# An AdaLN transformer block on one core: the last layernorm transposed by VectorE and DMAs, both down projections of the first batch in a row, and two more warm-up tiles

## Chip, cores and metric

The kernel runs on one core of one Trainium2 chip. The metric is the device time of one execution in microseconds. The reading units are the five engines of the core: TensorE (PE, with its weight loads as PEld), VectorE (DVE), ScalarE (ACT), GpSimd (POOL) and SyncE (SP, which here only issues DMAs).

## The reference

Two batches of 1024 rows of 256 numbers go through an attention block and a feed-forward block, both behind a layernorm that a small product of the condition `c` shifts and scales. Everything is float32. There are 16 heads of 128, causal masking, and a hidden size of 704 in the feed-forward part.

```python
mod = (silu(c) @ wmod).reshape(2, 6, 1, 256)
sa, ca, ga, sb, cb, gb = (mod[:, i] for i in range(6))
ga = (2 * (ga >= 0) - 1) * maximum(abs(ga), 0.25)       # gb likewise
h = layernorm(x) * (1 + ca) + sa
x = x + ga * attention(h, Wq, bq, Wk, bk, Wv, bv, Wo, bo)   # rotary q and k, causal
h = layernorm(x) * (1 + cb) + sb
gate, up = h @ Wgate.T, h @ Wup.T                       # W = (wq - 128) * scale per row
x = x + gb * ((silu(gate) * up) @ Wdown.T)
```

## The kernel before

All of it is written out by hand in one order: within `tc.manual_schedule()` each engine executes its instructions as the program emits them, and the framework adds only the semaphores. So the place of a call in the text is its place in the queue of every engine that it uses.

**Start.** `warm_up(n)` issues one product of a matrix of ones into a scratch bank of PSUM (`warm_ps`), n tiles of 128 columns wide; nobody reads it. There is one `warm_up(4)` before the condition arrives, and `warm_up(4)` and `warm_up(2)` behind the tiny transpose `pc` of the condition. Then `modulation(0)` multiplies the condition with the weights `wmod` (tile `pm`, line 125) as they land, and `ln_turn` transposes the first layernormed rows on TensorE (tile `ptx_a`, line 218); `gates_product` (`pg`) and the projections `pq`, `pk`, `pv` follow.

**Middle.** 32 units, one for each batch and head, are computed one after the other. A unit has eight steps of 128 query rows: scores (`ps`), softmax, and the probabilities turned. That turning is done without TensorE: VectorE transposes 32x32 blocks into the buffer `t32[blk]`, and 16 DMAs from SP move the blocks to their places in `pT` (tags `pT0` and `pT1`). The products with the values (`po`), the output projection (`py`) and the next unit's q, k, v are put between the steps. `project_out` multiplies one row tile and VectorE adds it to `x` (line 521).

**Layernorm.** It consists of `ln_stats`, `ln_sqrt` and `ln_scale` (result `xn`), and then one of two ways to turn rows into columns. `ln_turn` uses eight TensorE transposes for each block of 512 rows, into PSUM, and VectorE applies shift and scale while draining. The other way, which the second batch's first layernorm and the first batch's second one use, is `ln_move` (VectorE, 32x32 blocks), `ln_send` (16 DMAs on SP for both blocks) and `ln_shift` (shift and scale on POOL). The last layernorm, the one of batch 1 before the feed-forward part, uses `ln_turn`.

**Feed-forward and tail.** For each batch `b` and block `blk` of 512 rows, `hidden(b, blk, c)` makes one of six chunks of 128 hidden features (tile `pgu`, in a pair of banks of the pool `ps_sc`), ScalarE applies silu, and VectorE multiplies gate and up into `gT`. With `hold=True` that multiplication is put off until the next `owed.pop()()`. The last chunk holds 64 gate and 64 up features. `down(b, blk)` multiplies `gT` with the down weights for four row tiles: `chunks` are the 128-row products (tile `pd`, line 606), `halves` the 64-row products of the last chunk (line 596), alternately from the upper and the lower half of the partitions. `store` adds `x` on VectorE (tile `yo`, line 622) and sends the rows out by SP (line 623). Before the change `halves` come after the chunks, except in the very last `down`, where they come first.

Late `py` tiles and the `pd` tiles take their bank from `bank()`, in rotation over four entries:

```python
banks = [(ps_y, "y"), (ps_a, "a"), (ps_a, "a"), (ps_o, "o")]
```

`ps_o` with its single bank also holds `po`, so `values` waits until the last late `py` there has been drained.

The tail after the 32 units is a plain sequence: the four chunks of hidden(0, 1) between the last output projections, the statistics of the first four row tiles of batch 1, the last `values`, then hidden(0, 1, 4), four projections, hidden(0, 1, 5), the transposes of block 0 of the last layernorm, down(0, 0), and hidden(1, 0) with the transposes of block 1 behind its first chunk and down(0, 1) behind its fourth; then hidden(1, 1) with down(1, 0) in it, and down(1, 1).

Of the kernel before, what the change touches and what calls it, by code (L numbers as in the profile page):

```python
# [11 lines left out]
F32 = mybir.dt.float32  # L12
# [5 lines left out]
P = 128  # L18
B, S, D = 2, 1024, 256
H, DH = 16, 128  # L20
HID = 704
NT = S // P
KC = D // P
HG = 2
NG = H // HG
NF = (HID + P - 1) // P
FULL = (HID // P) * P
QB = 512
NB = S // QB
# [8 lines left out]
def adaln_block(ctx: ExitStack, tc: tile.TileContext, a, cos_d, sin_d, out):  # L38
    nc = tc.nc
# [7 lines left out]
    ps_a = pool("ps_a", 2, space=PSUM)  # L47
    ps_o = pool("ps_o", 1, space=PSUM)
    ps_y = pool("ps_y", 1, space=PSUM)
# [36 lines left out]
    def warm_up(tiles):  # L86
        some = ones.unsqueeze(1).to_broadcast([P, tiles, P])
        nc.tensor.matmul(warm_ps[:, : tiles * P], ones, some, start=True, stop=True)
# [108 lines left out]
    def ln_scale(b, name, blk, part=range(4)):  # L197
        mv, rstd = stats[b, name]
        part = [4 * blk + j for j in part]
        some = slice(part[0], part[-1] + 1)  # L200
        nc.vector.reciprocal(rstd[:, some], rstd[:, some])
        for t in part:
            xn = xnp.tile([P, D], F32, tag="xn", name=f"xn_{name}{b}_{t}")
            nc.vector.tensor_scalar(
                xn, x[b][:, t, :], mv[:, t, 0:1], rstd[:, t : t + 1], ALU.subtract, ALU.mult
            )
            xns[b, name, t] = xn
# [19 lines left out]

    moved = {}

    def ln_move(b, name, t):  # L230

        if t == 0:
            moved[b, name] = [
                fpool.tile([P, 4, NB, KC, 4, 32], F32, tag="f", name=f"xt{n}_{name}{b}") for n in range(2)
            ]

        nc.vector.transpose(
            moved[b, name][0][:, :, t // 4, :, t % 4, :].rearrange("p c f q -> p f c q"),
            xns[b, name, t].rearrange("p (f c a) -> p f c a", c=4, a=32),
        )  # L240

    def ln_send(b, name, cs):
        src, dst = moved[b, name]
        for c in cs:
            for r in range(4):
                nc.sync.dma_start(dst[ts(c, 32), r], src[ts(r, 32), c])

    def ln_shift(b, name, blk, which, dest, f):
        nc.gpsimd.tensor_scalar(
# [231 lines left out]
    def values(u, blk, k0, k1):  # L481
        b, g, h = u
        if blk == 0 and k0 == 0:
            outs[u] = opool.tile([P, S], F32, tag="o", name=f"o_{b}{g}{h}")
        if k0 == 0:
            pos[u, blk] = ps_o.tile([P, 512], F32, tag="o", name=f"po_{b}{g}{h}{blk}")
        po = pos[u, blk]
        last = 4 * blk + 3
        pT = pTs[u, blk].rearrange("p r i k b -> p i r k b")
        for k in range(k0, k1):  # L490
            off = max(0, k - 4 * blk)
            nc.tensor.matmul(  # L492
                po[:, off * P :],
                vs[b, g][:, k, ts(h, DH)],
                pT[:, off:, :, k, :],
                start=(k == 0),
                stop=(k == last),
            )
        if k1 == last + 1:
            nc.scalar.copy(outs[u][:, ts(blk, QB)], po)  # L500

    banks = [(ps_y, "y"), (ps_a, "a"), (ps_a, "a"), (ps_o, "o")]
    turn = [0]

    def bank(name):

        pool, tag = banks[turn[0] % 4]
        turn[0] += 1
        return pool.tile([P, 512], F32, tag=tag, name=name)

    def project_out(u, t, late=False):

        b, g, h = u
        if t % 4 == 0:
            nc.vector.reciprocal(rdens[u][:, t : t + 4], dens[u][:, t : t + 4])
        name = f"py_{b}{g}{h}{t}"
        py = bank(name) if late else ps_y.tile([P, 512], F32, tag="y", name=name)
        nc.tensor.matmul(  # L518
            py[:, :D], outs[u][:, ts(t, P)], weights[b, g]["o"][:, h, :], start=True, stop=True
        )  # L520
        nc.vector.scalar_tensor_tensor(  # L521
            x[b][:, t, :], py[:, :D], rdens[u][:, t : t + 1], x[b][:, t, :], ALU.mult, ALU.add
        )
# [4 lines left out]
    def new_h2(b, blk):  # L528

        tag = (f"hT{blk}", f"cs{blk}")[b]  # L530
        h2s[b, blk] = hpool.tile([P, KC, QB], F32, tag=tag, name=f"h2_{b}{blk}")
        return h2s[b, blk]

    def hidden(b, blk, c, late=True, first=None, hold=False):
        if c == 0 if first is None else first:
            gTs[b, blk] = fpool.tile([P, NF, QB], F32, tag="f", name=f"gT_{b}{blk}")
        last = c == NF - 1
        if late:
            pg = ps_sc.tile([P, S], F32, tag="sc", name=f"pgu_{b}{blk}{c}")
            pgs = [pg[:, ts(j, QB)] for j in range(2)]  # L540
        else:
            pgs = [
                ps_a.tile([P, 512], F32, tag="a", name=f"pgu_{b}{blk}{c}{j}") for j in range(2 - last)
            ]
        for pg, n in zip(pgs, ("gate",) if last else ("gate", "up")):
            for k in range(KC):
                nc.tensor.matmul(  # L547
                    pg,
                    wT["last"][:, k, :] if last else wT[n][:, k, ts(c, P)],
                    h2s[b, blk][:, k, :],  # L550
                    start=(k == 0),
                    stop=(k == KC - 1),
                )
        sg = ppool.tile([P, QB], F32, tag="p", name=f"sg_{b}{blk}{c}")

        rest = (last_gate_up if last else full_gate_up)(b, blk, c, sg, pgs)
        if hold:
            owed.append(rest)
        else:
            rest()  # L560
# [19 lines left out]
        nc.scalar.activation(sg, pgs[0], AF.Silu)  # L580
        return lambda: nc.vector.tensor_tensor(gTs[b, blk][:, c, :], sg, pgs[1], ALU.mult)

    def down(b, blk):

        end = (b, blk) == (1, 1)
        pds = [bank(f"pd_{b}{blk}{j}") for j in range(4)]

        parts = [(j, pds[j], slice(0, D)) for j in range(4)]
        if end:
            rest = ps_sc.tile([P, S], F32, tag="sc", name=f"pd_{b}{blk}r")  # L590
            parts[3:] = [(3, pds[3], slice(0, P)), (3, rest, slice(P, D))]

        def halves():
            for j, pd, cols in parts:
                half = ts(j % 2, HID - FULL)
                nc.tensor.matmul(  # L596
                    pd[:, cols],
                    gTs[b, blk][half, NF - 1, ts(j, P)],
                    wdT[b][half, NF - 1, cols],
                    start=end,  # L600
                    stop=not end,
                )

        def chunks(j, pd, cols):
            for c in range(NF - 1):
                nc.tensor.matmul(  # L606
                    pd[:, cols],
                    gTs[b, blk][:, c, ts(j, P)],
                    wdT[b][:, c, cols],
                    start=(c == 0 and not end),  # L610
                    stop=(c == NF - 2 and end),
                )

        def store(j, pd, cols):
            t = blk * 4 + j
            if cols.start == 0:
                if (b, blk) == (0, 0):
                    yos[t] = rot.tile([P, D], F32, tag="r1", name=f"yo_{b}{t}")
                else:
                    yos[t] = xnp.tile([P, D], F32, tag="xn", name=f"yo_{b}{t}")  # L620
            yo = yos[t]
            nc.vector.tensor_tensor(yo[:, cols], pd[:, cols], x[b][:, t, cols], ALU.add)
            nc.sync.dma_start(out[b, ts(t, P), cols], yo[:, cols])

        yos = {}
        if end:

            halves()
            for part in parts:
                chunks(*part)  # L630
                store(*part)
            return
        for part in parts:
            chunks(*part)
        halves()
        for part in parts:
            store(*part)
# [62 lines left out]
    with tc.manual_schedule():  # L700
        pc = ps_a.tile([P, 512], F32, tag="a", name="pc")
        nc.tensor.transpose(pc[:, : B * KC], row_c, ident[: B * KC, : B * KC])
        warm_up(4)
        warm_up(2)
        nc.scalar.activation(sc.rearrange("p b k -> p (b k)"), pc[:, : B * KC], AF.Silu)
        nc.scalar.activation(warm, eps_t, AF.Sqrt)
        weights[0, 0] = {}
# [97 lines left out]
            ln_stats(1, "b", t)  # L805
        ln_sqrt(1, "b", 0, 4)
        values(u, 1, 0, 8)
        ln_scale(1, "b", 0)
        hidden(0, 1, 4)
        for t in range(4, NT):  # L810
            project_out(u, t, late=True)
        hidden(0, 1, 5)
        ln_turn(1, "b", 0, 2, new_h2(1, 0), wide=True)
        for t in range(4, NT):
            ln_stats(1, "b", t)
        ln_sqrt(1, "b", 4, NT)
        ln_scale(1, "b", 1)
        down(0, 0)
        for c in range(NF):
            hidden(1, 0, c)  # L820
            if c == 0:
                ln_turn(1, "b", 1, 2, new_h2(1, 1))
            if c == 3:
                down(0, 1)
        order = (NF - 1, *range(NF - 1))
        for c in order:
            hidden(1, 1, c, first=(c == order[0]))
# [69 lines left out]
```

## Time and profile before

| | us |
|---|---|
| three runs, median (lowest to highest) | 1075.6 (1075.38 to 1075.73) |
| the profiled execution, its own time | 1076.84 |
| its span, first to last instruction | 1075.1 |

| engine | busy us | share of the span | instructions |
|---|---|---|---|
| PE | 1070.5 | 100% | 3529 |
| DVE | 655.1 | 61% | 1423 |
| ACT | 507.7 | 47% | 956 |
| POOL | 396.1 | 37% | 364 |

The page shows one profiled execution. Busy time is the time that an engine has an instruction in it; a float32 product of TensorE is recorded as two matmul instructions, and consecutive matmuls overlap in the records by their pipeline's depth (0.16 us at full speed), so that what one product costs in a row of them is read from the distance of the starts, or from the chain of work that ended last, which counts each instruction up to the next. Register, branch and DMA-issuing instructions are not counted as busy. A wait is put down to the last semaphore event before it.

### The profile page before, as it was taken

Reading aid. Unit: us, or ns where it says so; the run is one execution under the profiler, and the core shown is the slowest. Engines: PE = TensorE matmul, PEld = TensorE weight load, DVE = VectorE, ACT = ScalarE, POOL = GpSimd, SP = SyncE. Lnnn points to the kernel's source line nnn. Section 1 sums busy time; section 2 is a strip of 40 time slices with the busy share of each in tenths; the row PEclk is TensorE's granted clock in tenths of the full one; section 3 lists DMA queues with packets and bytes.
Section 4 is the critical chain, followed back from the end, with each engine's and each line's share of the span. In section 5 each row is a group of like instructions: output and inputs, shape, how many; then the busy total and the mean of one; then the engine's idle time right before and its main releaser. Section 6 shows DMA issues by size and latency. Waiting matters only on the chain.

```text
span 1075.1 us, 12364 instructions
## 1 busy us (share of the span) xinstructions
PE 1070.5 (100%) x3529; PEld 641.4 (60%) x3529; DVE 655.1 (61%) x1423; ACT 507.7 (47%) x956; POOL 396.1 (37%) x364
## 2 busy tenths in 40 slices
PE   9999999999999999999999999999999999999998
PEld 5656555666666655555666656655555666555656
DVE  5656665666767776665666566666677765544421
ACT  4654544554445544544554444444454554562110
POOL 3825353534343343754332443324343433100000
PEclk9999999999999999999999999999999999999999
DMA  6465655657565555565554656454555556432001
GB/s 218 96 161 126 161 119 135 164 127 181 118 152 112 142 117 134 122 149 126 112 148 109 147 113 155 101 139 99 139 114 126 143 128 137 103 69 49 20 20 40
DMA packets 66656, 130.99 MB, mean 122 GB/s; under 512 B 18806, under 2 KB 22010, under 8 KB 66588
## 3 DMA queue, kind: packets, MB, share of 16 engines
q1 hardware_dynamic: 64804, 125.78, 49.4%
q10 hardware_dynamic: 1736, 4.29, 1.2%
q8 instruction: 29, 0.48, 0.2%
q14 instruction: 39, 0.32, 0.1%
q0 software_dynamic: 48, 0.13, 0.1%
HBM read 25.26 MB, written 2.10 MB: 25 GB/s over the span
## 4 chain that ended last, share of the span: by engine, by line
PE 99%; DMA 0%; DVE 0%; SPq 0%; issue 0%
PE po L492 23%; PE ps L431 23%; PE pv L370 10%; PE pq L388 10%; PE py L518 10%; PE pk L388 10%; PE pgu L547 7%; PE pd L606 3%; PE pm L125 1%; DMA wmod<-in_wmod 0%; PE pd L596 0%; PE ptx_a L218 0%; PE pg L149 0%; PE ptx_b L218 0%; PE pd_11r L606 0%; DVE x L521 0%
## 5 line engine op out<-in xcount | busy, mean ns | idle before, releaser
L451 ACT ACTIVATE p<-ps,nmax 128x128 f32<-128x128 f32 (+7 forms) x256 | 189.8, 741 | 342.7 <-DVE nmax L434 342.3
L431 PE MATMUL ps<-kT,qT 128*128 128x512 f32 (+3 forms) x768 | 289.5, 486 | 0.0
L434 DVE CUSTOM_DVE_ANT_0 ps<-ps,mask 128x128 f32<-128x128 f32 (+7 forms) x256 | 195.5, 764 | 114.5 <-PE ps L431 113.6
L492 PE MATMUL po<-pT,v 128*128 128x512 f32 (+3 forms) x768 | 263.7, 486 | 0.1
L521 DVE SCALAR_TENSOR_TENSOR x<-py,rden,x 128x256 f32<-128x256 f32 x256 | 122.7, 481 | 220.6 <-PE py L518 216.8
L492 PEld LDWEIGHTS po<-pT,v 128*128 128x128 f32 x768 | 145.7, 190 | 123.9 <-issue 92.8
L401 POOL TENSOR_TENSOR r_q<-r_q,sin_t 128x512 f32<-128x512 f32 x64 | 81.9, 1280 | 364.5 <-ACT r_q L400 348.9
L465 DVE STREAM_TRANSPOSE t<-p 128x128 f32<-128x128 f32 (+7 forms) x256 | 198.2, 774 | 3.6 <-DMA pT<-t 1.8
L431 PEld LDWEIGHTS ps<-kT,qT 128*128 128x128 f32 x768 | 145.7, 190 | 77.6 <-issue 64.1
L518 PE MATMUL py<-wo,o 128*128 128x256 f32 x512 | 151.2, 380 | 0.0
L518 PEld LDWEIGHTS py<-wo,o 128*128 128x128 f32 x512 | 92.6, 190 | 77.6 <-issue 53.1
L370 PE MATMUL pv<-wv,hT 128*128 128x256 f32 x512 | 121.1, 379 | 0.0
L388 PE MATMUL pq<-hT,wq 128*128 128x512 f32 x256 | 120.5, 593 | 0.0
L388 PE MATMUL pk<-hT,wk 128*128 128x512 f32 x256 | 120.3, 592 | 0.0
L370 PEld LDWEIGHTS pv<-wv,hT 128*128 128x128 f32 x512 | 94.8, 190 | 19.5 <-issue 1.3
L401 POOL TENSOR_TENSOR r_k<-r_k,sin_t 128x512 f32<-128x512 f32 x64 | 81.5, 1273 | 64.4 <-ACT r_k L400 64.4
L407 POOL TENSOR_TENSOR kT<-kT,r_k 128x512 f32<-128x512 f32 x64 | 81.2, 1269 | 55.8 <-DVE kT L404 41.1
L400 ACT ACTIVATE r_q<-pq,cols 64x512 f32<-64x512 f32 x128 | 87.4, 683 | 22.3 <-PE pq L388 19.8
L407 POOL TENSOR_TENSOR qT<-qT,r_q 128x512 f32<-128x512 f32 x64 | 83.7, 1308 | 33.9 <-DVE qT L404 29.7
L400 ACT ACTIVATE r_k<-pk,cols 64x512 f32<-64x512 f32 x128 | 87.4, 683 | 6.4 <-PE pk L388 1.0
L388 PEld LDWEIGHTS pk<-hT,wk 128*128 128x128 f32 x256 | 48.6, 190 | 48.0 <-issue 44.2
L388 PEld LDWEIGHTS pq<-hT,wq 128*128 128x128 f32 x256 | 46.2, 190 | 33.1 <-issue 30.6
(96 smaller groups left out, 691.3 us busy)
## 6 DMA issues: line engine op xcount, KB each, us to landing
pT<-t SPq DMA_DIRECT2D x512, 128.0 KB, 2.4
pT<-t SPq DMA_DIRECT2D x512, 64.0 KB, 2.0
wq<-in_Wq SPq DMA_DIRECT2D x16, 256.0 KB, 3.0
wk<-in_Wk SPq DMA_DIRECT2D x16, 256.0 KB, 4.1
wv<-in_Wv SPq DMA_DIRECT2D x16, 256.0 KB, 4.1
wo<-in_Wo SPq DMA_DIRECT2D x16, 256.0 KB, 2.9
out<-yo SPq DMA_DIRECT2D x15, 128.0 KB, 1.8
wmod<-in_wmod SPq DMA_DIRECT2D x4, 256.0 KB, 5.5
```

The costliest lines, as they stand in the source:

```text
L370: nc.tensor.matmul(pv[:, ts(j, HG * DH)], hT[b, n][:, k, ts(r, P)], weights[b, g]["v"][:, k, :], start=(k == 0), stop=(k == KC - 1),)
L388: nc.tensor.matmul(pq, weights[b, g][s][:, k, ts(h, DH)], hT[b, n][:, k, :], start=(k == 0), stop=(k == KC - 1),)
L400: nc.scalar.activation(r1[to], pq[of], AF.Identity, bias=cols[of, c : c + 1])
L401: nc.gpsimd.tensor_tensor(r1, r1, sin_t[:, sl], ALU.mult)
L407: nc.gpsimd.tensor_tensor(dst[:, sl], dst[:, sl], r1, ALU.add)
L431: nc.tensor.matmul(ps[:, c:e], qT[:, ts(i, P)], kT[:, c:e], start=True, stop=True)
L434: nc.vector.tensor_tensor_reduce(ps[:, :L], ps[:, :L], mask[:, NT - 1 - i :, :].rearrange("p t k -> p (t k)"), -SCALE, FLT_MAX, ALU.add, A ...
L451: nc.scalar.activation(p[:, :L], ps[:, :L], AF.Exp, bias=nmax, scale=-1.0, accum_out=dens[u][:, i : i + 1])
L465: nc.vector.transpose(t32[blk][:, :, j, : i + 1, :].rearrange("p c k b -> p k c b"), p[:, : (i + 1) * P].rearrange("p (k c a) -> p k c a", ...
L492: nc.tensor.matmul(po[:, off * P :], vs[b, g][:, k, ts(h, DH)], pT[:, off:, :, k, :], start=(k == 0), stop=(k == last),)
L518: nc.tensor.matmul(py[:, :D], outs[u][:, ts(t, P)], weights[b, g]["o"][:, h, :], start=True, stop=True)
L521: nc.vector.scalar_tensor_tensor(x[b][:, t, :], py[:, :D], rdens[u][:, t : t + 1], x[b][:, t, :], ALU.mult, ALU.add)
```

## The change

- The last layernorm (batch 1, before the feed-forward part) is turned by `ln_move`, `ln_send` and `ln_shift` instead of `ln_turn`. `ln_move` gets buffers from the caller: the block transposes go into `t32[0]`, and a new tile in the pool slot `pT0` receives the DMAs. `ln_send` can send one block alone: 16 DMAs for block 0 behind the first four block transposes, and 16 more for block 1 behind down(0, 0)'s stores. In all there are 32 DMAs of 32 partitions x 256 elements, eight block transposes and four POOL instructions; 16 TensorE transposes and four VectorE drains go.
- down(0, 1) moves from behind hidden(1, 0, 3) to right behind down(0, 0). It takes two pairs of banks of `ps_sc` (`wide`) and does its 64-row products first (`first`), so that the 64-row products of down(0, 0) and down(0, 1) stand together.
- The multiplication of hidden(0, 1, 4) is held until the four output projections have been emitted.
- In the rotation of banks the third and the fourth entry change places.
- The two warm-up products behind `pc` are both four tiles wide: eight tiles instead of six.

```diff
-    def ln_move(b, name, t):
+    def ln_move(b, name, t, room=None):
         if t == 0:
-            moved[b, name] = [
+            moved[b, name] = room or [
...
-    def ln_send(b, name, cs):
+    def ln_send(b, name, cs, blks=slice(NB)):
         src, dst = moved[b, name]
         for c in cs:
             for r in range(4):
-                nc.sync.dma_start(dst[ts(c, 32), r], src[ts(r, 32), c])
+                nc.sync.dma_start(dst[ts(c, 32), r, blks], src[ts(r, 32), c, blks])
...
-    banks = [(ps_y, "y"), (ps_a, "a"), (ps_a, "a"), (ps_o, "o")]
+    banks = [(ps_y, "y"), (ps_a, "a"), (ps_o, "o"), (ps_a, "a")]
...
-    def down(b, blk):
+    def down(b, blk, wide=False, first=False):
         end = (b, blk) == (1, 1)
-        pds = [bank(f"pd_{b}{blk}{j}") for j in range(4)]
+        first = first or end
+        if wide:
+            pairs = [ps_sc.tile([P, S], F32, tag="sc", name=f"pd_{b}{blk}{j}") for j in range(2)]
+            pds = [pair[:, ts(j, QB)] for j in range(2) for pair in pairs]
+        else:
+            pds = [bank(f"pd_{b}{blk}{j}") for j in range(4)]
...
-                    start=end,
-                    stop=not end,
+                    start=first,
+                    stop=not first,
...
-        if end:
+        if first:
             halves()
...
-        warm_up(4)
-        warm_up(2)
+        for n in range(2):
+            warm_up(4)
...
         values(u, 1, 0, 8)
+        room = [t32[0], ptpool.tile([P, 4, 4, 4, 32], F32, tag="pT0", name="xt_b1")]
+        room = [
+            t.rearrange("p c a b q -> p (c a b q)").rearrange(
+                "p (c n f j q) -> p c n f j q", c=4, n=NB, f=KC, j=4
+            )
+            for t in room
+        ]
         ln_scale(1, "b", 0)
-        hidden(0, 1, 4)
+        for t in range(4):
+            ln_move(1, "b", t, room)
+        ln_send(1, "b", range(4), slice(0, 1))
+        hidden(0, 1, 4, hold=True)
         for t in range(4, NT):
             project_out(u, t, late=True)
+        owed.pop()()
         hidden(0, 1, 5)
-        ln_turn(1, "b", 0, 2, new_h2(1, 0), wide=True)
         for t in range(4, NT):
             ln_stats(1, "b", t)
         ln_sqrt(1, "b", 4, NT)
         ln_scale(1, "b", 1)
+        for t in range(4, NT):
+            ln_move(1, "b", t)
         down(0, 0)
+        for f in range(KC):
+            ln_shift(1, "b", 0, 2, h2s[1, 0] if f else new_h2(1, 0), f)
+        ln_send(1, "b", range(4), slice(1, 2))
+        down(0, 1, wide=True, first=True)
+        for f in range(KC):
+            ln_shift(1, "b", 1, 2, h2s[1, 1] if f else new_h2(1, 1), f)
         for c in range(NF):
             hidden(1, 0, c)
-            if c == 0:
-                ln_turn(1, "b", 1, 2, new_h2(1, 1))
-            if c == 3:
-                down(0, 1)
```

More of the change, by code (lines that the diff above doesn't have):

```diff
@@ L609, in chunks @@
                     wdT[b][:, c, cols],
-                    start=(c == 0 and not end),
-                    stop=(c == NF - 2 and end),
+                    start=(c == 0 and not first),
+                    stop=(c == NF - 2 and first),
                 )
```

## The prediction

> **What bounds the kernel now.** I read the page's engine table first, then the chain that ended last, then the timelines of the first 22 us and of the last 120 us. The page says that TensorE (PE) is the bound:
>
> ```profile
> span 1075.1 us, 12364 instructions
> PE 1070.5 (100%) x3529; PEld 641.4 (60%) x3529; DVE 655.1 (61%) x1423; ACT 507.7 (47%) x956; POOL 396.1 (37%) x364
> ```
>
> No other engine is above 61%. So a PE product taken away is worth its full pitch, and work given to DVE, POOL or SP costs nothing until PE waits for it. The chain over the last 136 us (start, duration, engine and tile; a product here is two matmul instructions) shows that PE hardly waits:
>
> ```profile
> 978.73 0.45 PE py L518 x2
> 979.18 0.03 issue
> 979.20 0.93 DVE x L521 x2
> 980.13 0.04 issue
> 980.17 5.86 PE po L492 x16
> ...
> 992.91 0.87 PE ptx_b L218 x8
> 993.78 8.63 PE pd L606 x40
> 1002.42 1.06 PE pd L596 x8
> 1003.48 3.63 PE pgu L547 x8
> 1007.11 0.87 PE ptx_b L218 x8
> ```
>
> The reader is to see three things. The eight transposes of each block (ptx_b) stand in the chain, at 0.109 us each. The 64-row products (L596) and the first hidden products behind them (3.63 us, where eight otherwise take 3.44) carry a surcharge. And one hop leaves PE: po waits for DVE's update of x.
>
> The other place is the start. In PE's timeline:
>
> ```profile
> 3.33 2.93 PE L88 MATMUL warm_ps<-ones 128*128 128x512 f32 x4
> 6.79 3.75 PE L125 MATMUL pm<-sc,wmod 128*128 128x128 f32 x16 [0.54 <-DMA wmod<-in_wmod]
> 10.33 1.45 PE L218 MATMUL ptx_a<-ident,xn_a 128*128 128x128 f32 x8
> ...
> 17.93 1.04 PE L218 MATMUL ptx_a<-ident,xn_a 128*128 128x128 f32 x8
> ```
>
> Sixteen pm instructions begin over 3.54 us, 0.213 us apart; the transposes at 17.93 are 0.109 apart. So PE runs at half speed until a switch. The eight transposes at 10.33 take 0.41 us more than their twins at 17.93, which is four slow ones (4 x 0.104): the switch is at about 10.33 + 4 x 0.213 = 11.2 us. The warm-ups stop 0.5 to 0.7 us before pm.
>
> **What the Trainium skill says.** (1) "TensorE: Matmul & The Clock Gate", Part 1: PE starts at half clock and is released after one busy window of about 3.4 us; windows run freely and do not restart with the kernel. The trace agrees on half and full pitch (0.213, 0.109); no view shows the windows themselves. (2) "TensorEngine Tiling (Array Packing)", Key Properties: a change of tiling mode drains TensorE. The trace agrees: a stretch of eight 64-row instructions costs 1.06 us and 0.19 on the products behind it, 1.25; they start as four pairs 0.209 apart (0.84), so entering and leaving costs 0.41. (3) "VectorE: DVE Perf Modes", The three transpose paths: VectorE transposes 32x32 blocks only, so DMAs must move the blocks; the kernel already does so for xt_a and xt_b, and its rows give the prices:
>
> ```profile
> L237 DVE STREAM_TRANSPOSE xt_b<-xn_b x8: 395/430/433, 814.6 to 855.1; 128x256 f32<-128x256 f32 x8
> L246 SPq DMA_DIRECT2D xt_a<-xt_a x16: 534/589/1371, 391.3 to 424.9; - x16
> L246 SPq DMA_DIRECT2D xt_b<-xt_b x16: 534/588/590, 860.2 to 893.9; - x16
> L249 POOL TENSOR_SCALAR h<-xt_b,modT x4: 769/772/779, 911.9 to 919.0; 128x512 f32<-128x512 f32 x4
> ```
>
> **The change, part by part.** Times below are the trace's, before any gain.
>
> *A. Transposes off PE.* 16 x 0.109 = **-1.75 us**, all in the chain. Their replacements: on DVE, 8 block transposes x 0.43 = 3.4 us, for four drains (4 x 0.8) that go. The first four stand behind the scaling (ends 985.2), end about 986.8, and are ahead of the four x updates, whose products come from 989.5: no delay. The hidden product held (hidden(0,1,4)) is multiplied after those updates, about 992.4; it is needed at 1003. The second four follow block 1's scaling (about 998.5 to 1000.2), write the half of t32_0 that the first sends do not read, and are done before the first store of down(0,0), about 1002.8. On SP, 16 sends x 0.588 = 9.4 us: 986.8 to 996.2, landing +2.0 (xt_b's landing), POOL 2 x 0.77: h2_10 is ready at 999.8. It is needed when hidden(1,0,0) begins: down(0,0) at 992.7, plus 8.63, plus 16 half products 2.1, plus 8.63, is 1012. Slack 12 us. Block 1: its sends wait on SP behind four output stores, of which two wait for a buffer (before: until 1005.4, end 1006.3); 1006.3 + 9.4 + 2.0 + 1.55 = 1019.3, needed at 1012 + 5.5 x 3.44 = 1031. Slack 11.6. The stores of down(0,1) queue behind these sends until about 1016; nobody waits, as their buffers are next written by down(1,0), some 30 us later. POOL has nothing else. The borrowed buffers are free: t32_0 and pT0 were last read for the po that ends at 965.8. Cost 0.
>
> *B. One stretch of half products less.* The two stretches cost 2 x 1.25 = 2.50; one of sixteen costs 8 x 0.209 + 0.41 = 2.08: **-0.42 us**. If the long stretch has its own extra drain between the two sets of banks, 0.2 of it is lost; no row shows this order. Two sc buffers serve as down(0,1)'s banks; their last readers end about 995, and the first is drained for hidden(1,0,0) while the last quarter of chunks (2.16 us) runs against a 0.42 us store.
>
> *C. Bank order.* po takes the bank that the second of three late py held (drained at 980.12). With o third in the list, it is the first of the three, drained at 979.69. From the pitches, po's second instruction stands 0.41 us late (two starts 0.53 apart where 0.43 is usual, after 0.31 of waiting). The release moves 0.43 earlier, but the weight load may still come 0.1 late: 0.25 to 0.41, I take **-0.33 us**. The later turns (down(0,0), down(1,0), down(1,1)) find banks drained long before.
>
> *D. Two warm-up tiles more.* At half clock they take 4 x 0.213 = 0.85 us: the warm-ups' issue ends at 6.90 instead of 6.05, wmod has landed at 6.65, so pm starts 0.1 later but its first, slower start (0.34) is gone: no loss. Gain, by the skill's window: if the switch at 11.2 closed a window, the ones before closed at 7.8 and 4.35; the window 4.35 to 7.8 held the gap of 0.5 to 0.7 us. Filled, it counts as busy, and PE is fast from 7.8. Then pm: 5 slow (to 7.95), 11 fast, done 9.15; the transposes wait for xn_a's fourth tile (DVE, 9.33) and end issuing at 10.05; pg 2 x 0.43 and its entry: pq starts at 11.1 instead of 12.66, **-1.55**. What could eat it: the second ptx_a would start at 16.4 and needs xn at 16.55 for its fourth tile: just in time; pq of block 1 at 20.1 needs hT from ACT (behind r_k, about 17.65, and the DVE drain): 20.05, just in time. The loads wq (about 9.4), wk (10.0) and wv (12.7) are there. I take **-1.5**. Bounds: +0.1 (the clock does not switch earlier) to -1.7 (half of 3.41).
>
> Sum: -1.75 - 0.42 - 0.33 - 1.5 = **-4.0 us**. The profiled execution takes 1076.84 (span 1075.1 and 1.7 around it), so 1072.8 profiled; the three other runs have a median of 1075.6, 1.2 less than the profiled one, so 1071.6.
>
> **The rivals.**
> *R1: the clock does not come early.* The windows run freely, so another execution can have another phase; or the busy share that the gate wants is met neither way. For it: a window that was busy for four fifths did not release PE. Against: the three runs agree within 0.35 us, which a random phase would hardly give. Then A to C alone: 1075.6 - 2.5 = 1073.1.
> *R2: a new wait gives back the tail.* DVE carries the stores of eight down tiles in a row, and two wait on output DMAs (1.6 us in the trace); if the last two slip behind hidden(1,0,0), PE waits 1 to 2.5 us: 1073 to 1075.5. Against: 1.3 us of cover per bank.
> *R3, slower: SP's sends.* Place: block 1's sends, behind block 0's sends and four stores. At x us a send, h2_11 is ready at 986.8 + 16x + 3 + 16x + 3.6 (3 for the stores that wait, 3.6 for landing and POOL) and wanted at 1031: late above x = 1.18. It outweighs 4.0 us by over 0.2% from x = 1.37, the longest single send in xt_a's row (1371 ns): then 6.3 late, 1077.9. Against: the median is 588 and all sixteen of xt_b lie under 591.
>
> **How the numbers follow.** 0.2% is 2.15 us, about what a measurement of this kernel can tell from no change. Forecast 0.64 (1071.0 to 1072.4), R1 0.22 (1072.7 to 1073.6; three quarters of it beyond 2.15), R2 0.08, R3 0.06. Faster: 0.64 + 0.17 + 0.02 = 0.83; same 0.11; slower 0.06. The likeliest time is 1071.6; the range 1071.0 to 1073.5 holds the forecast and most of R1.
>
> **What would show it.** Right: no ptx_b of batch 1 in the chain; one L601 stretch of 16 for batch 0, about 1.9 us; po's weight load waiting under 0.2 us for x; pm's start-to-start pitch falling from 0.213 to 0.109 within its sixteen, and pq starting near 11. Wrong: pm slow to its end (R1); a PE wait for yo at hidden(1,0,0) (R2) or for POOL's h before either hidden block (R3); any time above 1073.6 says that a step of A to C failed.

## The result, and the profile after

Twenty runs of each kernel, side by side: after 1074.55 us (median; 1072.97 to 1076.44), before 1075.99 us (1075.38 to 1077.83). The ratio is 0.998, with a 95% interval of 0.9973 to 0.9987: the changed kernel is faster by about 2.15 us (1.4 to 2.9). The ratio goes with the means, which lie 2.18 us apart; the medians lie only 1.44 apart, for a reason that follows. The forecast was 1071.6, in a range of 1071.0 to 1073.5. The sign was right; the size and the range were not.

The runs of both kernels fall into two groups, which matters for everything below. In these twenty, the ten lower times of before have a median of 1075.72 us and those of after 1073.20, 2.5 less; the ten upper ones 1077.29 and 1074.88, 2.4 less. So about half of the runs of either kernel stood in an upper group. The groups are clearest in the span of each run, without what lies around it. (Of these twenty, spans are known for after alone; those of before are from the runs beside e1 to e4, on one chip, and beside e5 to e8, on another.) I call a run late if its span is 1074.9 or more with the old tail, or 1072.5 or more with the new one:

| kernel | runs | early ones, their median span | late ones, their median span |
|---|---|---|---|
| before (beside e1 to e4) | 30 | 16, 1073.85 | 14, 1075.45 |
| before (beside e5 to e8) | 39 | 29, 1074.0 | 10, 1075.2 |
| after | 20 | 10, 1071.4 | 10, 1072.95 |
| e1: before, eight warm-up tiles | 13 | 7, 1073.8 | 6, 1075.1 |
| e2: after, six warm-up tiles | 9 | 6, 1071.3 | 3, 1072.8 |
| e3: after, scaling moved | 6 | 6, 1071.6 | 0 |
| e5: before, scaling moved | 13 | 11, 1073.9 | 2, 1075.0 |
| e6: before, eight tiles, scaling moved | 13 | 13, 1073.8 | 0 |
| e7: after, one product a step later | 10 | 10, 1071.25 | 0 |
| e8: after, six tiles, scaling moved | 14 | 14, 1071.4 | 0 |

The limits were drawn where the spans leave a gap. Read across, the new tail is worth 2.4 to 2.6 us in the early groups (before to e2; e1 to after; e5 to e8). The two extra tiles are worth nothing that shows (before to e1; e2 to after; e5 to e6: 0.1 either way). And a late run loses 1.1 to 1.6 us, which neither part of the change takes away: with the tiles alone 6 of 13 runs are late, with the tail alone 3 of 9.

The profiled executions were 1076.84 before and 1074.62 after. Both are late ones, for different reasons, as will be seen. The page's first lines, after:

```profile
span 1072.6 us, 12387 instructions
PE 1067.6 (100%) x3513; PEld 638.1 (59%) x3513; DVE 656.7 (61%) x1427; ACT 508.8 (47%) x956; POOL 399.2 (37%) x368
```

PE has 16 instructions fewer (the transposes) and 2.9 us less busy time; what moved to DVE and POOL changed neither into a bound. The chain that ended last, from the late output projections on (start, duration, engine, tile and line; `down` has moved by five lines, so L611 and L601 are L606 and L596 of before):

```profile
978.80 1.29 PE py L518 x6
980.10 5.59 PE po L492 x16
...
992.56 8.63 PE pd L611 x40
1001.20 1.93 PE pd L601 x16
1003.12 8.83 PE pd L611 x40
1011.96 31.09 PE pgu L547 x72
```

No ptx_b, no update of x by DVE, one stretch of 64-row products, and PE never leaves the chain. From the first of these py to PE's last instruction the tail took 93.56 us before (978.73 to 1072.29) and 91.00 after (978.80 to 1069.80): 2.56 less.

The start, in PE's timeline:

```profile
6.90 2.21 PE L125 MATMUL pm<-sc,wmod 128*128 128x128 f32 x16
...
10.86 1.98 PE L388 MATMUL pq<-hT,wq 128*128 128x512 f32 x4
```

Here too the forecast came true: pm follows the warm-ups without a wait, its pitch (from one start to the next) falls from 0.213 to 0.112 us at the third instruction (7.4 us), and pq starts at 10.86 instead of 12.66, 1.80 earlier. The next transposes then wait for xn; the second pg starts at 17.51 where it started at 18.89 before. What is left, 1.38 us, I call PE's lead.

At 254 us PE still has that lead: py starts at 253.48 in after and at 254.87 in before. At the next py 0.2 of it is left (257.46 and 257.67), and at the one behind that nothing (260.74 and 260.68). PE, DVE and POOL in the timeline there, after:

```profile
253.48 0.59 PE L518 MATMUL py<-wo,o 128*128 128x256 f32 x2
...
254.76 0.42 DVE L296 TENSOR_TENSOR sd<-s_down,gb 128x256 f32<-128x256 f32 x1 [2.08 <-DMA s_down<-in_scales]
255.20 1.27 POOL L401 TENSOR_TENSOR r_q<-r_q,sin_t 128x512 f32<-128x512 f32 x1 [12.34 <-ACT r_q L400]
255.22 1.79 DVE L297 SCALAR_TENSOR_TENSOR wdT<-raw_down,sd 128x512 f32<-128x512 int32 x1
256.93 0.47 DVE L521 SCALAR_TENSOR_TENSOR x<-py,rden,x 128x256 f32<-128x256 f32 x1
...
257.46 0.70 PE L518 MATMUL py<-wo,o 128*128 128x256 f32 x2 [1.02 <-DVE x L521]
```

And before, where PE was late already:

```profile
254.87 0.59 PE L518 MATMUL py<-wo,o 128*128 128x256 f32 x2
...
256.16 0.69 DVE L297 SCALAR_TENSOR_TENSOR wdT<-raw_down,sd 128x512 f32<-128x512 int32 x1
256.58 1.40 POOL L401 TENSOR_TENSOR r_q<-r_q,sin_t 128x512 f32<-128x512 f32 x1 [12.34 <-ACT r_q L400]
```

This is step 1 of unit 8: `ffn_down_scale` scales the first down weights (line 297) as soon as their scales have landed. It is an ordinary piece of the middle that the change does not touch. After, POOL's product of r_q began 0.02 us before DVE's scaling, and the scaling took 1.79 us instead of 0.69. The update of x behind it came late, and with it the one bank `ps_y` for the next py. The Trainium skill, "SBUF — State Buffer", section "SBUF: two separate sides", says that VectorE and GpSimd share a pair of ports as an exclusive lock: whoever starts first holds it for the whole instruction, and a VectorE operation with two SBUF inputs is among those concerned. The durations agree: 1.79 is 0.69 and most of POOL's 1.27 on top of each other. An estimate from these lines: with 0.69 for the scaling, the update of x and the py behind it would have started 1.1 us earlier, py at 256.36, and 1.3 of the lead would have been left.

So the profile offers this reading: the clock came early as forecast, and a chance meeting of two instructions, 250 us later, took the gain back. What the experiments had to tell is whether that was a cost of the change, and why the timed runs of before were 1.2 us below its profile.

### The profile page after: what moved, and what is told of

Its sections match the earlier page's. It is cut to its first block, busy times and chain, and to the rows that moved or that the text cites. A ratio compares the mean times of both kernels' runs of the same rounds, so it can differ in the third digit from the quotient of the medians.

```text
span 1072.6 us, 12387 instructions
## 1 busy us (share of the span) xinstructions
PE 1067.6 (100%) x3513; PEld 638.1 (59%) x3513; DVE 656.7 (61%) x1427; ACT 508.8 (47%) x956; POOL 399.2 (37%) x368
## 4 chain that ended last, share of the span: by engine, by line
PE 98%; DMA 1%; DVE 0%; issue 0%; ACT 0%; POOL 0%; ACTq 0%; POOLq 0%
PE ps L431 23%; PE po L492 23%; PE pk L388 10%; PE py L518 10%; PE pq L388 10%; PE pv L370 10%; PE pgu L547 7%; PE pd L611 3%; DMA s_down<-in_scales 1%; PE warm_ps L88 1%; PE pd L601 0%; PE pm L125 0%; PE ptx_a L218 0%; PE pg L149 0%; DVE ps L434 0%
```

## The experiments

**My theory:** the tail gives its 2.5 us in every run; the two tiles give about 1.4, and the meeting at 255 us takes it back wherever it happens. **Rival 1:** the tiles give nothing, because PE's clock comes early with six as well, and the profiled execution of before was an exception. **Rival 2:** the tail lost something to a new wait.

**e1, the two tiles alone.** On the kernel before:

```diff
-        warm_up(4)
-        warm_up(2)
+        for n in range(2):
+            warm_up(4)
```

> The kernel before with only the eight warm-up tiles (two products of four tiles behind pc instead of four and two). Theory A (clock gate with a free-running window): executions of the kernel before are of two kinds, those in which a busy window happens to end within the first warm-ups and TensorE is fast before pm (about 1075.5 us), and those in which the gap of 0.5 to 0.7 us before pm spoils the window and TensorE stays slow until about 10 to 13.6 us (1076.3 to 1077.8 us). Eight tiles close the gap, so the second kind goes: in this run's profile the pm products fall to a pitch of 0.11 us by 7.8 us at the latest, lowest time still 1075.4 us, and none above 1077.2. Theory B (the start's gain is lost at the scaling of the down weights near 255 us): part of the executions stand at 1076.8 to 1077.0 all the same, so the median moves by no more than 0.7 us. Rival (the start is worth its full 1.4 us in every execution): median 1.4 us below before, lowest about 1074.

Measured: 1075.99 us (median of 13), ratio 0.9998 (0.999 to 1.0006). Nothing gained. Its profile (1077.0) shows the clock early (7.7 us) and the meeting again:

```profile
255.28 1.27 POOL L401 TENSOR_TENSOR r_q<-r_q,sin_t 128x512 f32<-128x512 f32 x1 [12.34 <-ACT r_q L400]
255.36 1.74 DVE L297 SCALAR_TENSOR_TENSOR wdT<-raw_down,sd 128x512 f32<-128x512 int32 x1
```

Two groups of 7 and 6 runs: about half are late. But the early ones are no faster than before's early ones (1073.8 against 1073.85), which speaks for rival 1.

**e2, the tail alone.** The changed kernel with the old warm-ups:

```diff
-        for n in range(2):
-            warm_up(4)
+        warm_up(4)
+        warm_up(2)
```

> The changed kernel with six warm-up tiles as before, so only the layernorm's turning, down's place and order and the bank rotation are changed. Theory A: the same two kinds of executions as before, each 2.5 us shorter (1.75 transposes, 0.42 one stretch of 64-row products, 0.33 to 0.41 bank): lowest about 1073.0, slow starts 1073.8 to 1075.3 us, median 2.2 to 2.6 us below before. From the start of unit 1's second half to the last unit, TensorE's starts agree with those of before within 0.1 us wherever both starts have the same phase. Rival (part of the tail's gain is lost to a new wait): median under 2 us below before.

Measured: 1073.40 us (9 runs), ratio 0.9976 (0.9967 to 0.9986). The tail alone does as well as the whole change (0.998, 0.9973 to 0.9987), as far as these intervals tell; its median is lower because 6 of 9 runs were early here, and 10 of 20 after. PE's timeline shows that in this execution the gap in front of pm did not keep the clock down:

```profile
6.76 2.43 PE L125 MATMUL pm<-sc,wmod 128*128 128x128 f32 x16 [0.51 <-DMA wmod<-in_wmod]
```

The same wait for wmod as before, 0.5 us, and yet pm is done after 2.43 us and not after 3.75. In this execution the scales landed earlier, and DVE went first:

```profile
254.70 0.69 DVE L297 SCALAR_TENSOR_TENSOR wdT<-raw_down,sd 128x512 f32<-128x512 int32 x1
255.26 1.27 POOL L401 TENSOR_TENSOR r_q<-r_q,sin_t 128x512 f32<-128x512 f32 x1 [12.34 <-ACT r_q L400]
```

No meeting, and the lead was kept to the end: 1073.02.

**e3, the scaling moved out of the way.** The changed kernel, with both batches' down weights scaled in unit 9, long after the load has landed. (The expectations of e3 and e7 call the scaling in-place; it reads `raw_down` and writes `wdT`.)

```diff
-        if n in (8, 9) and i in (1, 3, 5):
-            ffn_down_scale(n - 8, i - 1)
+        if n == 9 and i < 6:
+            ffn_down_scale(i % 2, i - i % 2)
```

> The changed kernel with the six scalings of the down weights (lines 296 and 297) all in unit 9, one in each of steps 0 to 5, instead of units 8 and 9, so that VectorE does not wait for the load of s_down in unit 8 and its in-place scaling does not start together with GpSimd's r_q. Theory B: the 1.4 us gained at the start is kept past 258 us and reaches the end; all runs stand near 1073.0 to 1073.6 us and the group at 1074.5 to 1075.1 us is gone; median about 1.3 us below the changed kernel, 2.8 us below before. Theory A alone (only the phase of the clock makes the two groups): the two groups stay as they are, median 1074.5. Rival (another place further on absorbs the lead): the lead is lost later than 258 us in the trace, median unchanged.

Measured: 1073.68 us (6 runs), ratio 0.9971 (0.9959 to 0.9984). No run is late by its span. The load itself took 8.4 us to land in the profiled execution, longer than in after, and cost nothing: py starts at 253.27 and 256.07, its usual 2.80 apart. What still scatters is the very end. In its profiled execution (1073.97) the late py starts at 977.13 us, where it starts at 978.73 before and at 978.80 after, so the lead was whole; but SP's waits of the last 15 us read

```profile
SPq L913 <- DMA out<-yo: 2.2, 1, 2.2
```

where the same row of after has 0.9: the last output rows landed 1.3 us later. It is the only one of the twelve profiled executions with more than 0.9 there. That is one more chance, of about the size of the effect under study.

**e4, no second warm-ups.** The kernel before without both calls:

```diff
-        warm_up(4)
-        warm_up(2)
```

> The kernel before with both warm-up products behind pc taken away, so TensorE is idle from about 3.4 us until wmod lands near 6.8 us. Theory A: no busy window can end before pm, so every execution is of the slow kind: pm and ptx_a at 0.213 us pitch until a switch between 10.2 and 13.6 us, times 1076.3 to 1077.9 us and no run at 1075.4 to 1075.7; median about 1 us above before. Rival (the two groups of before have nothing to do with the clock): a group at 1075.4 to 1075.7 us remains.

Measured: 1077.09 us (13 runs; spans from 1074.7, median 1075.2), ratio 1.0007 (0.9999 to 1.0015). None of its runs reaches before's early group beside it, which ends at 1074.2. In its profile PE idles 3.18 us ahead of pm, and pm is slow to its end:

```profile
6.57 3.76 PE L125 MATMUL pm<-sc,wmod 128*128 128x128 f32 x16 [3.18 <-DMA wmod<-in_wmod]
```

(The scales took 8.7 us there as well, so that this execution is late twice over, the second slowest of its 13.) So the warm-ups do work, by about 1.3 us of span against before's early group. The ratio alone does not show it, as before's late runs lie where these do. But six tiles are enough for it in most runs.

**e5 and e6, the start without the meeting.** The kernel before with e3's edit (e5), and with e3's and e1's (e6).

> The kernel before with the six scalings of the down weights moved into unit 9, so that nothing of them stands behind the load in unit 8. What is left of the start's two kinds must then be the clock alone. Theory A (the gap of 0.5 to 0.7 us in the warm-ups makes some executions start late): two groups, about 1075.2 to 1075.6 us (switch of pitch before 7.8 us) and 1076.4 to 1077.3 us (after 10 us), the profile's own switch telling to which its time belongs. Theory B alone (all of before's upper group comes from the collision near 255 us): only the lower group is left, median 1075.4. Single executions about 1.3 us longer by a late landing of the last stores occur in either.

> The kernel before with eight warm-up tiles and the scalings in unit 9. Theory A with B: every execution is fast by 7.8 us and keeps its lead of 1.4 to 1.6 us past 258 us, so nearly all times lie at 1075.0 to 1075.7 us, median 0.5 to 0.9 us below before; those above are late landings of the last stores (about +1.3). Rival (the warm-ups do nothing, the switch follows from elsewhere): same distribution as the kernel before with the late scalings and six tiles.

Measured: e5 1075.71 us (13 runs), ratio 1.0 (0.9992 to 1.0008); e6 1075.63 (13), ratio 0.9998 (0.9989 to 1.0006). The 0.5 to 0.9 us expected of e6 did not come. By spans, the early runs of e5 and e6 differ by 0.1; e5 has 2 late runs in 13 and e6 none, too few to tell apart. This speaks for rival 1 once more: with six tiles, too, the clock seems to come early in most runs. The traces show it in four of five profiled executions; in e5's, pm takes 2.33 us behind a wait of 0.39 for wmod.

**e7, one product a step later.** The changed kernel; DVE still waits for the scales where it did, but the first scaling goes to the end of step 2:

```diff
-    def ffn_down_scale(b, c):
+    def ffn_down_scale(b, c, part=""):
-        if c == 0:
+        if c == 0 and part != "w":
...
+        if part == "sd":
+            return
...
-        if n in (8, 9) and i in (1, 3, 5):
+        if n == 8 and i in (1, 2):
+            ffn_down_scale(0, 0, ("sd", "w")[i - 1])
+        elif n in (8, 9) and i in (1, 3, 5):
```

> The changed kernel with one piece moved: in unit 8 the product sd = s_down x gate stays in step 1 (and still waits for the load), but the first in-place scaling of wdT goes to the end of step 2. It tells the wait for the load from the collision of the scaling with GpSimd's r_q. If the collision costs the lead: VectorE's x update follows sd directly, TensorE's py waits at most 0.3 us, the lead at 260 us is 1.1 us or more, and the group at 1074.5 to 1075.1 us thins out, median near 1073.3. If the wait for the load costs it: sd ends about 255.2 and py still starts about 257.4 or the lead is gone elsewhere in unit 8; times as the changed kernel's, median 1074.5.

Measured: **1073.05 us** (10 runs, 1072.85 to 1073.65), ratio 0.9975 (0.9966 to 0.9984). No late run, and the least scatter of all. Its timeline (line numbers two higher):

```profile
254.76 0.42 DVE L296 TENSOR_TENSOR sd<-s_down,gb 128x256 f32<-128x256 f32 x1 [1.92 <-DMA s_down<-in_scales]
255.11 0.48 DVE L523 SCALAR_TENSOR_TENSOR x<-py,rden,x 128x256 f32<-128x256 f32 x1
...
256.97 0.68 DVE L299 SCALAR_TENSOR_TENSOR wdT<-raw_down,sd 128x512 f32<-128x512 int32 x1
```

The wait for the scales is as in after, and sd starts at the same 254.76; but the meeting is gone. The update of x comes at 255.11 instead of 256.93, POOL's r_q runs undisturbed from 255.36 to 256.64, and py starts at 256.45 instead of 257.46, without a wait. So waiting for the scales until 254.76 does not cost the lead by itself. The trace is not after's with the meeting alone taken away, though: POOL started 0.16 us later here, so that even in the old place the scaling might have gone first. The timed runs carry more: none of 10 is late, where 10 of the 39 runs of before beside them are. By the ratio e7 is 2.7 us faster than before. Its median is the lowest of the versions run, 1.5 below after's, but after was timed on another occasion, when half of before's runs, too, stood in the upper group; between the early groups of the two, 0.15 remains.

**e8, e7's question with six tiles.** The changed kernel with e2's and e3's edits.

> The changed kernel with six warm-up tiles and the scalings in unit 9: with the run that has eight tiles and late scalings it tells what the two more tiles are worth where the lead isn't lost later. Theory A: two groups, 1072.7 to 1073.2 us and 1073.9 to 1074.8 us, in the shares of the kernel before; with eight tiles only the lower. Rival (the phase seldom falls badly, six tiles are enough): nearly all at 1072.7 to 1073.2, as with eight.

Measured: 1073.28 us (14 runs, 13 of them under 1073.9), ratio 0.9974 (0.9967 to 0.9982). With the meeting gone, six tiles do as well as eight within what these runs can tell (spans 1071.4 and, in e7, 1071.25). In its profiled execution the scales took 8.7 us to land, and py kept its 2.80. On the chip of e5 to e8, 10 of 39 runs of before were late, against 2 of 50 of these four kernels.

**e9, the bank order alone** (a single run):

```diff
-    banks = [(ps_y, "y"), (ps_a, "a"), (ps_a, "a"), (ps_o, "o")]
+    banks = [(ps_y, "y"), (ps_a, "a"), (ps_o, "o"), (ps_a, "a")]
```

> The kernel before with only the bank rotation changed (third and fourth entry). As the prediction sized it: po of the last unit's values stands 0.25 to 0.41 us sooner behind the py tiles than in the kernel before (start of po's second instruction less start of the last py: 1.06 us there, 0.65 to 0.8 here), and nothing else in the tail moves against the kernel before. Rival (the update of x is late anyway): no change at po, 1.06 us.

Measured: 1077.12 us, 1077.21 for before beside it. The place itself, in the chain:

```profile
979.42 1.30 PE py L518 x6
980.72 5.59 PE po L492 x16
```

Here po starts straight behind the last py, as in after. The hop over DVE is gone, and po's second start follows the last py by 0.645 us instead of 1.059: 0.41 gained. The time is a late one for another reason: clock early, no meeting, but the scales landed so late that DVE itself was stuck.

```profile
256.48 0.42 DVE L296 TENSOR_TENSOR sd<-s_down,gb 128x256 f32<-128x256 f32 x1 [3.71 <-DMA s_down<-in_scales]
...
258.08 0.70 PE L518 MATMUL py<-wo,o 128*128 128x256 f32 x2 [1.55 <-DVE x L521]
```

So a late landing (9.4 us after the issue) can take the lead by itself. By this reading e7's edit, which still waits for the scales in step 1, would not have helped there; e3's would, as e3 and e8 kept the lead with landings of 8.4 and 8.7.

**e10, the two down products apart again** (a single run). The changed kernel with down(0, 1) in its old place, with its old banks and its 64-row products last:

```diff
-        down(0, 1, wide=True, first=True)
...
         for c in range(NF):
             hidden(1, 0, c)
+            if c == 3:
+                down(0, 1)
```

> The changed kernel with down(0, 1) back behind hidden(1, 0, 3), in the rotating banks and with its 64-row products last, so that two stretches of eight 64-row instructions stand apart again. As sized: TensorE's tail is 0.42 us longer than in the changed kernel from the start of down(0, 0) to the start of hidden(1, 1)'s second chunk, all of it at the ends of the two stretches. Rival (moving the products cost a wait of its own in the changed kernel, which goes here): less than 0.3 us longer, or shorter.

Measured: 1073.16 us (before beside it 1077.21, a late run). The chain:

```profile
990.83 8.63 PE pd L611 x40
999.47 1.06 PE pd L601 x8
...
1023.09 1.06 PE pd L601 x8
```

From the first pd to the one of down(1, 0) it takes 50.88 us (990.83 to 1041.71), and in after 50.48 (992.56 to 1043.04): bringing the stretches together is worth 0.40.

## Why the prediction was right about the tail and wrong about the time

**A, transposes off PE: right.** PE's starts after each of the two places moved up by the eight transposes, 0.87 and 0.88 us (the gaps they leave in the chain of before), 1.75 in all, and nothing paid for it. The sends, the block transposes and the shifts in the trace after:

```profile
L246 SPq DMA_DIRECT2D xt_b<-t x32: 507/589/1342, 986.7 to 1014.9; - x32
L249 POOL TENSOR_SCALAR h<-xt_b,modT x8: 768/768/771, 911.9 to 1017.7; 128x512 f32<-128x512 f32 x8
```

SP began at 986.7 as worked out. POOL's last two instructions end at 1018.5, with h2_11 forecast for 1019.3. One send took 1342 ns, close to the 1371 on which R3 was built; the median of 589 decided.

**B: right.** 0.40 in e10, and 0.40 between the starts of after and before (50.48 against 51.76 less the 0.88 of the transposes), for 0.42. The drain is what "TensorEngine Tiling (Array Packing)", Key Properties, speaks of; no view shows the drain itself, only its cost: the sixteen took 1.93 us and left 0.20 on the products behind them (8.83 instead of 8.63), 2.13 for the 2.08 worked out.

**C: right, and under-sized.** 0.41 (e9, and between the traces of before and after) for 0.33: the upper bound was the value.

A to C were to give 2.5. They gave 2.56 in the traces, and 2.4 to 2.6 between the early groups. Of R2 and R3 there is no trace: PE waits for nothing between 980 and 1043 us. So the last sign of the forecast was wrong, that a time above 1073.6 would say that a step of A to C had failed: after's median is above it, and none had.

**D, the warm-ups: the step that failed, at its size.** Within the profiled pair it was even too small at the start (1.80 for 1.55), and the xn wait it named cut it to 1.38. The error lies in what it was taken from. The profiled execution of before had a slow clock until 11.2 us, and I wrote that the timed runs were 1.24 us below it, then carried the 1.24 over as an offset of the whole sum. But that offset *was*, by all that the runs show, the late clock: the profiled execution of before is late by its clock alone, and e5's, with an early clock and no meeting, took 1075.83, within 0.25 of the three runs' median. So the sum counted the same 1.24 twice, once as D's gain and once as the offset. In most of the runs that were timed the clock had come early already, and of the 1.5 there was 0.1 to gain (e5 and e6). The sum against the timed median would have been 2.5 plus 0.1, 1073.0, where after's early runs lie (nine at 1072.97 to 1073.97, and one at 1074.85 whose span is early).

That the filled gap is what brought the clock early in after is not shown either: in e2, with a gap of 0.51, PE is fast from 7.6 us, about when it is in after (7.4) and e1 (7.7), which have none.

The argument against R1 failed with it. I took the agreement of three runs, within 0.35 us, as a sign that the phase of the clock's windows is the same each time. It is not. And that all three fell into the lower group was luck: they are the first three of the twenty, of which half lie above. PE becomes fast at these times (read from its pitch and from the clock that the profile records), with the start of the second pg:

| execution | tiles | PE fast from, us | second pg starts |
|---|---|---|---|
| before | 6 | 11.2 | 18.89 |
| e9 | 6 | 4.8 | 17.60 |
| e8 | 6 | 6.2 | 17.98 |
| e5 | 6 | 7.3 | 17.88 |
| e2 | 6 | 7.6 | 17.58 |
| e10 | 8 | 4.8 | 17.24 |
| e6 | 8 | 5.0 | 17.58 |
| e7 | 8 | 5.0 | 17.68 |
| e3 | 8 | 5.7 | 17.30 |
| after | 8 | 7.4 | 17.51 |
| e1 | 8 | 7.7 | 17.60 |
| e4 | 2 | 12.3 | 19.28 |

The switch falls anywhere between 4.8 and 7.7, or, in two executions, at 11.2 and 12.3. In six of the twelve it comes before pm has begun, so there neither the gap in front of pm nor its filling could matter to it. "TensorE: Matmul & The Clock Gate", Part 1, says just this: windows run freely, and how many products are slow varies from run to run. No view here shows the windows, only the switch. What hides the phase is DVE: pq starts at 10.8 to 11.05 in all the early ones, and the second transposes wait for xn. Runs agree because a cover evens them out, not because the clock does.

R1's time, 1073.1, is where the early runs lie, but its reason was right by half: another execution has another phase, but the clock then mostly comes early, with either kernel. R2's band, 1073 to 1075.5, holds the median, and its wait never occurred.

**What no step had.** Half of after's runs are late, by about 1.6 us of span, which puts its median at the lower edge of the late group and above the range. The range held only what the change could do; it had no term for a lottery that before has too, and whose losing side before's own profile, 1.24 above the median, had shown in one execution of four. Whether PE keeps its lead at 255 us hangs on when the scales land. With the scaling in its old place they took 7.80 us in after and 7.85 in e1 (met), 7.2 in e2 and 7.1 in e10 (missed), and 9.4 in e9 (too late without a meeting). Whether the change makes the meeting more likely is open: 10 of 20 runs are late after, where half of before's twenty beside them stand in the upper group too; before is late in 24 of the 69 beside e1 to e8, of which some are late by the clock. What made a run late (late clock, meeting, late scales) is shown for the profiled ones alone; for the timed ones it is argued from the late runs becoming rare when the scaling is moved, 2 in 56 (e3, e5 to e8).

## What to carry to other kernels

Before an effect is sized from a profiled execution, set its time against the median: a difference as large as the effect means that this execution is perhaps the exception which the edit would cure. When runs fall into two groups, compare group with group and count, as a median jumps by the whole gap when one run changes sides. A product with two SBUF inputs on VectorE is best put where GpSimd is not about to start: with one such instruction moved by a step no run of ten was late, while two more warm-up tiles left the late runs as they were.

## What the runs showed of the hardware

- Where the scaling on VectorE and r_q on GpSimd started within 0.1 us of each other, they ran almost one after the other: the scaling took 1.74 to 1.79 us behind POOL instead of 0.69. It holds the other way round as well. In e1, 13 us later, both start together, and now POOL is the one that waits (1.82 instead of 1.27). The recorded starts do not tell who goes first when they lie so close: POOL's is 0.01 us earlier here, and in after, at 268.16 us, it is earlier by the same 0.01 and DVE waits (1.80).

```profile
268.25 1.82 POOL L401 TENSOR_TENSOR r_q<-r_q,sin_t 128x512 f32<-128x512 f32 x1
268.26 0.68 DVE L297 SCALAR_TENSOR_TENSOR wdT<-raw_down,sd 128x512 f32<-128x512 int32 x1
```

- PE was fast before pm ended in ten of the twelve profiled executions, with waits of up to 1.24 us in front of pm; with 3.18 us (e4), and once with 0.54 (before), it was not. How busy PE must be to become fast is not settled by these runs.
- One and the same load took 7.1 to 9.4 us to land from execution to execution, and the landing of the last stores moved the end by 1.3 us in one of the twelve (e3), with no edit near either. Below 0.2% such scatter is as large as what one tunes.
